# Two-layer model on one core: expert row transfers spread over half steps, routing one batch at a time, and one batch's results fetched at another step

## The chip, the cores and the metric

The kernel runs on one core of one Trainium2 chip. It is written by hand for the core's engines: PE (matrix products into PSUM), VectorE (DVE), ScalarE (ACT), GpSimd (POOL), and SyncE (SP), which here issues most DMA transfers. Each engine works through its own instructions in order; semaphores tie the engines together. The metric is device time in microseconds (us) of one execution.

## The reference

Four batches of 512 tokens with 128 features go through two layers. Each layer normalizes the tokens, computes attention `s` and a feed-forward gate `g` from the same normalized tokens, and adds `s * silu(g)`:

```python
x = L0_attn_x                                  # (4, 512, 128)
xn = _layernorm(x)
s = _L0_attn_ref(xn, ...)   # 16 heads, recurrent over 8 segments of 64 tokens, memory and softmax
g = _silu(_L0_ffn_ref(xn, ...))                # 8 experts, 2 of them per token, and a shared one
x = x + s * g
xn = _layernorm(x)
s = _L1_attn_ref(xn, ...)   # 16 heads of 8, softmax attention summed over 16 channels
g = _silu(_L1_ffn_ref(xn, ...))
x = x + s * g
```

The second layer's experts are what this change is about. Every token takes the two experts with the highest probability, with those two probabilities as weights:

```python
g = gelu(xt @ wg1 + bg1); logits = g @ wg2
probs = softmax(logits); top_vals, top_idx = top_k(probs, 2)
gates = zeros.at[row, top_idx].set(top_vals)
h = gelu(einsum('nd,edh->enh', xt, w_in))      # 8 experts, 128 -> 256
o = einsum('enh,ehd->end', h, w_out)           # 256 -> 128
y = einsum('ne,end->nd', gates, o)
```

## The kernel before

The kernel computes the second layer's experts by rows. It doesn't run all 8 experts over all tokens; it copies each token's row to the two places in DRAM that belong to its two experts, runs each expert over its rows, and fetches each token's two results back. Two halves are treated apart: batches 0 and 1, and batches 2 and 3. An expert has room for 512 rows in each half, so there are 16 pairs of half and expert, called experts 0 to 15 below.

The stages in order of time, by the trace:

- loading, first normalization and the first layer's experts, to about 100 us;
- attention of the first layer (`attn0`), 32 segment steps n, to 422.9 us. The loop runs `attend(n)` and `attended(n - 1)` in each step, and calls what a dictionary `between` holds: an entry n - 0.5 before `attend(n)`, an entry n after `attended(n - 1)`. So work of the second layer's routing is written into steps 18 to 30.5;
- the second layer's experts by rows (`ffn1`), 16 steps i, 422.9 to about 531 us. A second dictionary `between` puts work into the steps: routing of batches 2 and 3, and the preparation (`prepare`) of the second attention's first batch;
- attention of the second layer (`attn1`), 64 steps i = 16 b + t (batch b, t from 0 to 15), 533 to 890 us, and the end.

The order of instructions on every engine is the order in which the program issues them (`pin` and the helpers `mm1`, `act1`, `vec1`, `pool1` and `dma1` record and keep it). So a position in the loop is a position in five queues. Line L322 is the helper of all matrix products, L325 of all ScalarE activations, L334 of transfers issued by SyncE: in the profile one must go by tile names.

The functions of the experts and their names in the profile:

- `sums`, `scale`, `normed`, `turned`: layer normalization of a batch and its transposes (`lnt`);
- `hidden`, `logits`, `chosen`, `placed`: the router of a batch (`pgr`, `lp`, `idx`, `rank`), which ends in `slots` (L1017), the DRAM rows that each token's two copies go to, and `found`, where its results will be;
- `sent(b)` (L1024): eight indirect transfers on GpSimd, four tiles of 128 tokens times two choices. Each scatters 128 rows of 512 bytes from `xn` to the half's DRAM region `in`;
- `fetched(i)`: a 256 KB load of expert i's rows from `in` into `xg` (two buffers), issued by SyncE;
- `faced(i)`: four PE transposes (`xgt`, L1045) and a ScalarE copy (`xt`);
- `up1(i)`: two matrix products (`ph`); `gelu1(i)`: the Gelu into `h` (three buffers in the pool `f1x`);
- `down1(i)`: 16 products (`eo`), a VectorE copy (`y`, L1071), and its 256 KB store to `out`.

The pool `f1x` is opened after `attn0`'s memory is given back, in the same addresses. In step i of `ffn1` before, the order is `up1(i)`, `gelu1(i)`, the entries of `between`, `faced(i + 1)`, `fetched` of a later expert, `down1(i - 1)`.

In `attn1`, at t = 8 of each batch, `back1` issues eight indirect fetches on GpSimd (L1135) from `out`, four for each choice, into `g` and a second tile `bk`. At t = 10 `together` weights and adds them on VectorE (L1145, L1146). At t = 12 `gate1` applies the gate. `zeros1` clears one of two sets of operand strips (L1335) on GpSimd, and `operands1` issues transfers that fill operands.

Of the kernel before, what the change touches and what calls it, by code (L numbers as in the profile page):

```python
# [98 lines left out]
class Kernel:  # L99
# [814 lines left out]
    def begin_ffn1(self, pool, psum, layer):  # L914
# [103 lines left out]
            self.vec1(v.tensor_scalar_min(self.found[:, tiles(b)], row, NE * ROOM - 1.0))  # L1018
            self.vec1(v.tensor_reduce(self.full[:, b : b + 1], rank, AX.XY, ALU.max))

        def sent(b):
            for k in range(4):
                for c in range(2):
                    self.pool1(nc.gpsimd.indirect_dma_start(  # L1024
                        out=self.places[b // 2][b % 2 * 8 + k * 2 + c],
                        out_offset=bass.IndirectOffsetOnAxis(
                            ap=self.slots[:, b * 4 + k, c : c + 1], axis=0
                        ),
                        in_=xn[b][k], in_offset=None,
                    ))  # L1030

        def rows_of(where, i):

# [21 lines left out]
                )  # L1055

        def gelu1(i):
            h = self.f1x.tile([P, 2, 4, P], F32, name=name("h", i), tag="h", bufs=3)
            self.act1(h.rearrange("p c k t -> p c (k t)"), out["h", i], AF.Gelu)
            out["h", i] = h  # L1060

# [46 lines left out]
    def ffn1(self, first, between):  # L1108


        n = 2 * NE
        for i in range(n):
            if i:
                first.up1(i)
            first.gelu1(i)
            for f, *args in between.get(i, []):
                f(*args)
            if i + 1 < n:
                first.faced(i + 1)

            for k in [i + 3] if i + 3 < NE else [NE, NE + 1] if i == NE - 2 else [i + 3] * (
                NE - 2 < i < n - 3
            ):
                first.fetched(k)
            if i:
                first.down1(i - 1)
        first.down1(n - 1)

    def back1(self, b):

        nc, acc = self.nc, self.of_batch("g", 1, b)
        other = self.a1.tile([P, 4, D], F32, name=f"bk{b}", tag="pr1", bufs=2)
        for c, t in enumerate((acc, other)):
            for k in range(4):
                self.pool1(nc.gpsimd.indirect_dma_start(  # L1135
                    out=t[:, k, :], out_offset=None, in_=self.rows_out[b // 2][:],
                    in_offset=bass.IndirectOffsetOnAxis(
                        ap=self.found[:, b * 4 + k, c : c + 1], axis=0
                    ),
                ))  # L1140

        def together():
            for k in range(4):
                w = self.share[:, b * 4 + k]
                self.vec1(nc.vector.tensor_scalar_mul(acc[:, k, :], acc[:, k, :], w[:, 0:1]))  # L1145
                self.vec1(nc.vector.scalar_tensor_tensor(  # L1146
                    acc[:, k, :], other[:, k, :], w[:, 1:2], acc[:, k, :], ALU.mult, ALU.add
                ))
        return acc, together
# [581 lines left out]
    def attn1(self, xnT, g1):  # L1731
# [4 lines left out]
        with tc.tile_pool(name="a1", bufs=2) as self.a1, tc.tile_pool(  # L1736
# [48 lines left out]

            steps = {9: 0, 11: 1, 13: 2, 1: 3}

            def features(b, t):

                out = [(0, t - 1)] if b == 0 and 1 <= t < 5 else []  # L1790
                if t in steps and (b, t) != (0, 1):
                    out.append((b + (t > 1), steps[t]))
                return out
            waiting, late, prep, products = [], [], {}, []
            large = self.large1(flag)
            for i in range(n):
                b, t = i // 16, i % 16
                if i == 0:
                    self.zeros1(1)
                if t == 8:  # L1800
                    g1[b], together = self.back1(b)
                if t == 12:
                    self.gate1(pool, g1[b], b)
                if t % 4 == 2:

                    m = t // 4 + 2
# [27 lines left out]
                    f()  # L1834
                if b == B - 1 and t in (3, 11):
                    large[t // 8]()
                if t == 10:
                    together()
                late = [f for f in [rest(x) for rest, x in ready] if f]
                if nxt:  # L1840
# [301 lines left out]
    def run(self):  # L2142
# [15 lines left out]
        with tc.tile_pool(name="wf1", bufs=1) as wf1, tc.tile_pool(name="f1", bufs=1) as f1:  # L2158
# [11 lines left out]
            with tc.tile_pool(name="ap", bufs=1, space=PSUM) as psum:  # L2170
# [5 lines left out]
                    21: [(first.turned, 0), (first.normed, 1)],  # L2176
                    22: [(first.turned, 1), (first.hidden, 0), (first.hidden, 1)],
                    23: [(first.logits, 0), (first.logits, 1), (first.chosen, 0)],
                    24: [(first.chosen, 1), (first.placed, 0)],
                    25: [(first.placed, 1), (first.sent, 0)], 26: [(first.sent, 1)],  # L2180
                    29: [(first.fetched, 0), (first.fetched, 1)], 30.5: [(first.faced, 0)],
                })
                left[0]()
                first.up1(0)
# [11 lines left out]
                with f1x as self.f1x:  # L2196
# [3 lines left out]
                    def prepare(k):  # L2200
# [2 lines left out]
                        rest(evict[0](ps) if evict else ps)  # L2203

                    self.ffn1(first, {
                        0: [(prepare, 2), (first.sums, 2), (first.sums, 3), (first.scale, 2, 4)],
                        1: [(prepare, 3), (first.normed, 2), (first.turned, 2)],
                        2: [(first.normed, 3), (first.turned, 3), (first.hidden, 2)],
                        3: [(first.hidden, 3), (first.logits, 2), (first.logits, 3),
                            (first.chosen, 2), (first.chosen, 3)],  # L2210
                        4: [(first.placed, 2), (first.sent, 2), (first.placed, 3),
                            (first.sent, 3)],
                        5: [(prepare, 0)], 7: [(prepare, 1), (prepare, 9)],
                        10: [(prepare, 4)], 11: [(prepare, 5)], 12: [(prepare, 6), (prepare, 7)],
                        13: [(prepare, 8)], 14: [(prepare, 10)],
                        15: [(self.opening1, psum, "w", 3)],
# [68 lines left out]
```

## Time and profile before

| what | value |
|---|---|
| median of 3 runs | 915.35 us (912.18 to 916.57) |
| the profiled execution | 915.94 us |
| its span, first to last instruction | 914.1 us |
| mean granted PE clock | 0.959 |
| PE, VectorE, ScalarE, GpSimd busy | 829.5, 594.6, 512.8, 461.6 us |

The profiled execution gives all durations below; it lies 0.6 us above the median. Busy time by stage shows that PE is nearly full everywhere but in the experts by rows:

```profile
core 0: us, PE busy (x) PEld busy (x) DVE busy (x) ACT busy (x) POOL busy (x), PEclk, DMA share, GB/s
0.00:80.00 80.00, 73.42 (x368) 45.97 (x370) 55.43 (x206) 28.42 (x52) 49.66 (x169) 1.00 0.56 155
...
100.00:422.90 322.90, 300.28 (x3595) 257.91 (x3595) 219.56 (x481) 176.34 (x292) 160.46 (x173) 0.96 0.18 52
422.90:533.00 110.10, 90.15 (x545) 63.53 (x545) 30.29 (x119) 37.45 (x47) 40.34 (x43) 0.91 0.32 105
533.00:890.00 357.00, 330.41 (x2612) 114.41 (x2616) 267.08 (x300) 257.31 (x282) 204.47 (x149) 0.97 0.28 87
```

Each row is a stretch of time (its start and end, its length), the busy time of each engine in it with the number of instructions in brackets, the granted PE clock, the mean busy share of the DMA engines and what they moved. The last three rows are the stages that the change touches: the first attention, the experts by rows, and the second attention. A matrix product at half clock takes up to twice its time and counts as busy all of it, so a full PE at a low clock isn't PE at its peak.

### The profile page before, as it was taken

Reading aid. Unit: us, or ns where it says so; the run is one execution under the profiler, and the core shown is the slowest. Engines: PE = TensorE matmul, PEld = TensorE weight load, DVE = VectorE, ACT = ScalarE, POOL = GpSimd, SP = SyncE. Lnnn points to the kernel's source line nnn. Section 1 sums busy time; section 2 is a strip of 40 time slices with the busy share of each in tenths; the row PEclk is TensorE's granted clock in tenths of the full one; section 3 lists DMA queues with packets and bytes.
Section 4 is the critical chain, followed back from the end, with each engine's and each line's share of the span. In section 5 each row is a group of like instructions: output and inputs, shape, how many; then the busy total and the mean of one; then the engine's idle time right before and its main releaser. Section 6 shows DMA issues by size and latency. Waiting matters only on the chain.

```text
span 914.1 us, 18790 instructions
## 1 busy us (share of the span) xinstructions
PE 829.5 (91%) x7428; PEld 505.9 (55%) x7428; DVE 594.6 (65%) x1152; ACT 512.8 (56%) x692; POOL 461.6 (50%) x540
## 2 busy tenths in 40 slices
PE   8998899999999979697968979969999999989896
PEld 4666789888898858585546732322334323422325
DVE  7774776766768785464332236856887887887684
ACT  3434565665656663343512258826776777678670
POOL 7660254454544433755454207973766586551512
PEclk9999999999999998878988999979999999999998
DMA  8822321212212120200523222532251225131000
GB/s 215 260 65 65 88 74 32 82 36 60 82 24 83 25 70 19 61 27 12 189 81 112 82 98 87 196 104 53 70 184 48 81 76 180 54 94 34 24 13 16
DMA packets 85791, 74.42 MB, mean 81 GB/s; under 512 B 41744, under 2 KB 66608, under 8 KB 85696
## 3 DMA queue, kind: packets, MB, share of 16 engines
q1 hardware_dynamic: 81456, 67.52, 24.4%
q0 software_dynamic: 3664, 5.36, 2.2%
q8 instruction: 61, 1.00, 0.4%
q14 instruction: 34, 0.28, 0.1%
q10 hardware_dynamic: 576, 0.26, 0.1%
HBM read 41.66 MB, written 31.46 MB: 80 GB/s over the span
## 4 chain that ended last, share of the span: by engine, by line
PE 64%; DVE 13%; issue 7%; DMA 6%; POOL 4%; ACT 4%; SPq 1%; another core or an unknown queue 1%; DVEq 0%; POOLq 0%; ACTq 0%
PE acc L322 9%; PE pp L322 6%; PE dot L322 6%; PE eo L322 5%; DVE e L1720 5%; PE po L322 5%; PE sc L322 4%; PE mm L322 3%; PE mu L322 3%; PE ph L322 3%; PE pv L322 2%; ACT e L325 2%; DMA other<-qe 2%; PE s L322 2%; PE pk L683 2%
## 5 line engine op out<-in xcount | busy, mean ns | idle before, releaser
L1720 DVE TENSOR_TENSOR e<-e,e 128x1024 f32<-128x1024 f32 x126 | 189.8, 1546 | 68.2 <-ACT e L325 68.1
L322 PE MATMUL acc<-e,strip 128*32 128x512 f32 x1520 | 189.1, 601 | 23.9 <-DVE e L1720 12.2
L325 ACT ACTIVATE e<-s 128x1024 f32<-128x1024 f32 x126 | 122.1, 1022 | 89.7 <-PE s L322 74.9
L325 ACT ACTIVATE e<-e 128x1024 f32<-128x1024 f32 x126 | 126.3, 1060 | 0.0
L322 PEld LDWEIGHTS acc<-e,strip 128*32 128x32 f32 x1520 | 44.6, 110 | 142.0 <-issue 87.2
L325 ACT ACTIVATE pj<-pp 128x512 f32<-128x512 f32 x64 | 38.2, 596 | 65.2 <-PE pp L322 57.5
L776 POOL TENSOR_TENSOR t<-t,gate 128x512 f32<-128x512 f32 x32 | 40.8, 1275 | 54.9 <-DVE t L709 40.2
L322 PE MATMUL dot<-vone,E 128*128 128x65 f32 x512 | 63.2, 277 | 0.6 <-issue 0.5
L322 PEld LDWEIGHTS dot<-vone,E 128*128 128x128 f32 x512 | 61.5, 196 | 1.5 <-issue 1.2
L728 POOL TENSOR_TENSOR t<-t,gate 128x512 f32<-128x512 f32 x32 | 40.9, 1279 | 33.5 <-DVE t L709 33.4
L751 DVE TENSOR_TENSOR mz<-mz,mu 64x512 f32<-64x512 f32 x56 | 38.4, 685 | 22.8 <-PE mu L322 17.4
L647 DVE TENSOR_TENSOR E<-sc,cap 128x1024 f32<-128x1024 f32 x32 | 39.0, 1220 | 16.2 <-PE sc L322 11.6
L325 ACT ACTIVATE attT<-pa 128x512 f32<-128x512 f32 x32 | 19.1, 597 | 54.1 <-PE pa L787 48.9
L671 DVE SCALAR_TENSOR_TENSOR elu<-elu,up 128x512 f32<-128x512 f32 x60 | 42.6, 710 | 7.2 <-ACT up L325 6.4
L1071 DVE COPY y<-eo 128x512 f32<-128x512 f32 x16 | 11.1, 691 | 55.5 <-PE eo L322 41.1
L325 ACT ACTIVATE h<-ph 128x1024 f32<-128x1024 f32 x16 | 16.4, 1024 | 53.5 <-PE ph L322 35.6
L777 POOL TENSOR_TENSOR t<-t,t 128x512 f32<-128x512 f32 x32 | 45.1, 1408 | 2.5
L1024 POOL DMA_INDIRECT in<-xn,slots x32 | 31.8, 995 | 27.0 <-DVE slots L1017 17.9
L744 POOL TENSOR_TENSOR mz<-mz,zs 64x8 f32<-64x8 f32 x56 | 11.7, 208 | 66.4 <-DVE zs L676 57.7
L322 PE MATMUL eo<-w_out,h 128*128 128x128 f32 x256 | 35.1, 295 | 10.1 <-DVE y L1071 8.6
L322 PE MATMUL s<-q,k 32*128 32x512 bf16 x512 | 39.9, 387 | 3.8 <-DMA q<-qd 3.0
L1568 POOL TENSOR_TENSOR pr<-pr,pr 128x512 f32<-128x512 f32 x14 | 21.5, 1552 | 41.7 <-DVE pr L1563 41.7
(303 smaller groups left out, 1771.8 us busy)
## 6 DMA issues: line engine op xcount, KB each, us to landing
vd<-vt SPq DMA_DIRECT2D x32, 256.0 KB
vone<-vd SPq DMA_DIRECT2D x64, 128.0 KB
in<-zero SPq DMA_DIRECT2D x2, 2048.0 KB
xg<-in SPq DMA_DIRECT2D x16, 256.0 KB
out<-y SPq DMA_DIRECT2D x16, 256.0 KB
k<-kd SPq DMA_DIRECT2D x16, 256.0 KB
q<-qd SPq DMA_DIRECT2D x16, 256.0 KB
rows<-qd SPq DMA_DIRECT2D x64, 64.0 KB
```

The lines of the kernel that those rows point to most:

```text
L322: return self.pin(self.nc.tensor.matmul(*args, **kw))
L325: return self.pin(self.nc.scalar.activation(*args, **kw))
L647: self.vec1(nc.vector.tensor_tensor(e.rearrange("p x hp c -> p (x hp) c"), ps.rearrange("p x hp c -> p (x hp) c"), bc(self.cap.rearrange(" ...
L671: self.vec1(nc.vector.scalar_tensor_tensor(t, t, 1.0, up, ALU.min, ALU.add))
L683: self.pin(nc.tensor.transpose(ps[:, hp], src[:, 2 * hp : 2 * hp + 2, :].rearrange("d a j -> d (a j)"), self.ident,))
L728: nc.gpsimd.tensor_mul(t, t, self.gate)
L751: self.vec1(nc.vector.tensor_tensor(new[half, :, :, p, 0:DK], old[half, :, :, p, 0:DK], ps[half, :, :, p * 64 : p * 64 + 64].rearrange("d ...
L776: nc.gpsimd.tensor_mul(t, t, gate2)
L777: nc.gpsimd.tensor_add(t, t, seg[n]["t1"])
L1024: self.pool1(nc.gpsimd.indirect_dma_start(out=self.places[b // 2][b % 2 * 8 + k * 2 + c], out_offset=bass.IndirectOffsetOnAxis(ap=self.slo ...
L1568: self.nc.gpsimd.tensor_add(self.prod1[b, m], self.prod1[b, m], t)
L1720: self.vec1(self.nc.vector.tensor_mul(t, src[0][pair], src[1][pair]))
```

## The change

It has seven parts.

1. In the first attention, the transfers of batches 0 and 1 are no longer issued eight at step 25 and eight at step 26, but two at each half step from 25.5 to 29. The loads of experts 0 and 1 move from step 29 to step 30.
2. The first Gelu's `h` gets memory of its own ("h0") in place of a buffer in `f1x`.
3. In a step of `ffn1`, `faced(i + 1)` comes ahead of the entries of `between`, and the load of a later expert comes after `down1(i - 1)`. Entries of i + 0.5 are called after that. Expert 8 (the first of the second half) is faced at the end of step 7. The loads of experts 8 and 9 move from step 6 to step 7, those of 10 and 11 to step 8.
4. Batches 2 and 3 are routed one after the other, each with its own eight transfers: batch 2's at step 3, batch 3's at step 4.5, where before all 16 were at step 4.
5. `bk` gets one buffer of its own tag; before it shared two buffers with products of the second attention.
6. Batch 0's results are fetched at i = 13, added at 15 and gated at 17, where before this was at 8, 10 and 12. The other batches keep their steps.
7. The clearing of the second operand set moves from the second attention's step 0 to step 9 of `ffn1`.

```diff
--- before.py
+++ after.py
@@ -1018,16 +1018,17 @@
             self.vec1(v.tensor_scalar_min(self.found[:, tiles(b)], row, NE * ROOM - 1.0))
             self.vec1(v.tensor_reduce(self.full[:, b : b + 1], rank, AX.XY, ALU.max))
 
-        def sent(b):
-            for k in range(4):
-                for c in range(2):
-                    self.pool1(nc.gpsimd.indirect_dma_start(
-                        out=self.places[b // 2][b % 2 * 8 + k * 2 + c],
-                        out_offset=bass.IndirectOffsetOnAxis(
-                            ap=self.slots[:, b * 4 + k, c : c + 1], axis=0
-                        ),
-                        in_=xn[b][k], in_offset=None,
-                    ))
+        def sent(b, first=0, end=8):
+
+            for n in range(first, end):
+                k, c = n // 2, n % 2
+                self.pool1(nc.gpsimd.indirect_dma_start(
+                    out=self.places[b // 2][b % 2 * 8 + n],
+                    out_offset=bass.IndirectOffsetOnAxis(
+                        ap=self.slots[:, b * 4 + k, c : c + 1], axis=0
+                    ),
+                    in_=xn[b][k], in_offset=None,
+                ))
 
         def rows_of(where, i):
 
@@ -1055,7 +1056,9 @@
                 )
 
         def gelu1(i):
-            h = self.f1x.tile([P, 2, 4, P], F32, name=name("h", i), tag="h", bufs=3)
+
+            where, tag, bufs = (self.f1x, "h", 3) if i else (pool, "h0", 1)
+            h = where.tile([P, 2, 4, P], F32, name=name("h", i), tag=tag, bufs=bufs)
             self.act1(h.rearrange("p c k t -> p c (k t)"), out["h", i], AF.Gelu)
             out["h", i] = h
 
@@ -1108,28 +1111,34 @@
     def ffn1(self, first, between):
 
 
+
         n = 2 * NE
         for i in range(n):
             if i:
                 first.up1(i)
             first.gelu1(i)
+            if i + 1 < n and i + 1 != NE:
+                first.faced(i + 1)
             for f, *args in between.get(i, []):
                 f(*args)
-            if i + 1 < n:
-                first.faced(i + 1)
-
-            for k in [i + 3] if i + 3 < NE else [NE, NE + 1] if i == NE - 2 else [i + 3] * (
-                NE - 2 < i < n - 3
-            ):
-                first.fetched(k)
             if i:
                 first.down1(i - 1)
+
+            if i + 3 < NE or NE < i < n - 3:
+                first.fetched(i + 3)
+            elif NE - 2 < i <= NE:
+                for k in range(2):
+                    first.fetched(2 * i - NE + 2 + k)
+            for f, *args in between.get(i + 0.5, []):
+                f(*args)
+            if i + 1 == NE:
+                first.faced(NE)
         first.down1(n - 1)
 
     def back1(self, b):
 
         nc, acc = self.nc, self.of_batch("g", 1, b)
-        other = self.a1.tile([P, 4, D], F32, name=f"bk{b}", tag="pr1", bufs=2)
+        other = self.a1.tile([P, 4, D], F32, name=f"bk{b}", tag="bk", bufs=1)
         for c, t in enumerate((acc, other)):
             for k in range(4):
                 self.pool1(nc.gpsimd.indirect_dma_start(
@@ -1785,6 +1794,8 @@
 
             steps = {9: 0, 11: 1, 13: 2, 1: 3}
 
+            back = {16 * b + 8: b for b in range(1, B)} | {13: 0}
+
             def features(b, t):
 
                 out = [(0, t - 1)] if b == 0 and 1 <= t < 5 else []
@@ -1795,12 +1806,12 @@
             large = self.large1(flag)
             for i in range(n):
                 b, t = i // 16, i % 16
-                if i == 0:
-                    self.zeros1(1)
-                if t == 8:
-                    g1[b], together = self.back1(b)
-                if t == 12:
-                    self.gate1(pool, g1[b], b)
+                if i in back:
+                    fb = back[i]
+                    g1[fb], together = self.back1(fb)
+                if i - 4 in back:
+                    fb = back[i - 4]
+                    self.gate1(pool, g1[fb], fb)
                 if t % 4 == 2:
 
                     m = t // 4 + 2
@@ -1834,7 +1845,7 @@
                     f()
                 if b == B - 1 and t in (3, 11):
                     large[t // 8]()
-                if t == 10:
+                if i - 2 in back:
                     together()
                 late = [f for f in [rest(x) for rest, x in ready] if f]
                 if nxt:
@@ -2176,9 +2187,12 @@
                     21: [(first.turned, 0), (first.normed, 1)],
                     22: [(first.turned, 1), (first.hidden, 0), (first.hidden, 1)],
                     23: [(first.logits, 0), (first.logits, 1), (first.chosen, 0)],
-                    24: [(first.chosen, 1), (first.placed, 0)],
-                    25: [(first.placed, 1), (first.sent, 0)], 26: [(first.sent, 1)],
-                    29: [(first.fetched, 0), (first.fetched, 1)], 30.5: [(first.faced, 0)],
+                    24: [(first.chosen, 1), (first.placed, 0)], 25: [(first.placed, 1)],
+                } | {
+                    25.5 + 0.5 * k: [(first.sent, k // 4, k % 4 * 2, k % 4 * 2 + 2)]
+                    for k in range(8)
+                } | {
+                    30: [(first.fetched, 0), (first.fetched, 1)], 30.5: [(first.faced, 0)],
                 })
                 left[0]()
                 first.up1(0)
@@ -2203,14 +2217,16 @@
                         rest(evict[0](ps) if evict else ps)
 
                     self.ffn1(first, {
-                        0: [(prepare, 2), (first.sums, 2), (first.sums, 3), (first.scale, 2, 4)],
-                        1: [(prepare, 3), (first.normed, 2), (first.turned, 2)],
-                        2: [(first.normed, 3), (first.turned, 3), (first.hidden, 2)],
-                        3: [(first.hidden, 3), (first.logits, 2), (first.logits, 3),
-                            (first.chosen, 2), (first.chosen, 3)],
-                        4: [(first.placed, 2), (first.sent, 2), (first.placed, 3),
-                            (first.sent, 3)],
+                        0: [(first.sums, 2), (first.sums, 3), (first.scale, 2, 4)],
+                        0.5: [(prepare, 2), (first.normed, 2), (first.turned, 2)],
+                        1: [(first.hidden, 2), (prepare, 3)],
+                        1.5: [(first.logits, 2), (first.normed, 3)],
+                        2: [(first.chosen, 2), (first.turned, 3)],
+                        2.5: [(first.hidden, 3)],
+                        3: [(first.placed, 2), (first.sent, 2), (first.logits, 3)],
+                        3.5: [(first.chosen, 3)], 4.5: [(first.placed, 3), (first.sent, 3)],
                         5: [(prepare, 0)], 7: [(prepare, 1), (prepare, 9)],
+                        9: [(self.zeros1, 1)],
                         10: [(prepare, 4)], 11: [(prepare, 5)], 12: [(prepare, 6), (prepare, 7)],
                         13: [(prepare, 8)], 14: [(prepare, 10)],
                         15: [(self.opening1, psum, "w", 3)],
```

## The prediction

> **What bounds the kernel now.** I read the page first, then the list of waits, then a table of stretches, then the timeline around two of them, then the chain of waits.
>
> ```profile
> span 914.1 us, 18790 instructions
> ...
> PEclk9999999999999998878988999979999999999998
> ...
> L1024 POOL DMA_INDIRECT in<-xn,slots x32 | 31.8, 995 | 27.0 <-DVE slots L1017 17.9
> ```
>
> PE is busy 91% of the span, so what a row of 40 slices can't show matters: where PE stands, and where its clock is low. The transfers of rows (L1024) are 32 instructions of 0.995 us on POOL. That row's sum, 31.8 us, is small. What happens around them isn't, as the list of waits shows (us in total, times, longest):
>
> ```profile
> POOL in L1024 <- DVE slots L1017: 17.9, 1, 17.9
> ...
> DVE y L1071 <- issue: 14.5, 2, 12.1
> ACT h L325 <- remote: 13.5, 1, 13.5
> ```
>
> POOL waits once 17.9 us for the slots of batch 2 and then issues 16 transfers. VectorE and ScalarE wait 12.1 and 13.5 us at one place for a releaser that the profile can't name ("issue", "remote"). The table of stretches shows where. They are, in order: the transfers of batch 0 and of batch 1 in the first attention, what follows each, the 16 transfers of batches 2 and 3 in the experts, the eight fetches of batch 0's results in the second attention, what follows, and batch 1's fetches for comparison.
>
> ```profile
> core 0: us, PE busy (x) PEld busy (x) DVE busy (x) ACT busy (x) POOL busy (x), PEclk, DMA share, GB/s
> 362.00:374.00 12.00, 6.67 (x80) 5.61 (x76) 5.31 (x9) 3.47 (x6) 9.65 (x11) 0.92 0.11 44
> 378.00:390.00 12.00, 8.60 (x89) 7.20 (x87) 6.23 (x14) 4.33 (x7) 9.67 (x11) 0.93 0.21 66
> 390.00:400.00 10.00, 9.60 (x70) 8.98 (x71) 7.31 (x14) 4.33 (x7) 6.42 (x8) 0.53 0.18 54
> 400.00:415.00 15.00, 14.47 (x196) 13.19 (x192) 11.99 (x25) 5.98 (x9) 7.42 (x8) 1.00 0.00 1
> 472.00:486.00 14.00, 5.42 (x27) 4.18 (x26) 0.69 (x1) 0.45 (x2) 11.46 (x14) 0.71 0.17 66
> 592.00:604.00 12.00, 8.81 (x72) 3.20 (x64) 2.71 (x5) 4.04 (x5) 8.39 (x8) 1.00 0.60 176
> 604.00:622.00 18.00, 12.24 (x48) 4.71 (x52) 14.43 (x24) 8.66 (x10) 10.53 (x6) 0.53 0.13 45
> 682.00:695.00 13.00, 12.60 (x111) 5.94 (x103) 10.26 (x19) 8.15 (x9) 10.14 (x8) 1.00 0.22 66
> ```
>
> In 400–415 PE is full at clock 1.00. In 362–374 and 378–390 it is busy 6.67 and 8.60 of 12 us, in 472–486 5.42 of 14, while POOL is busy with transfers all along, and after them the clock is about half (0.53 in 390–400 and in 604–622). Batch 1's fetches (682–695) leave PE 12.60 of 13 us; batch 0's, with a DMA share of 0.60 against 0.22, don't. The timeline says what ends these stands:
>
> ```profile
> 481.96 0.97 POOL L1024 DMA_INDIRECT in<-xn,slots  x1 [0.30 <-issue]
> 482.81 0.69 DVE L1071 COPY y<-eo 128x512 f32<-128x512 f32 x1 [12.09 <-issue]
> ...
> 485.68 1.02 ACT L325 ACTIVATE h<-ph 128x1024 f32<-128x1024 f32 x1 [13.55 <-remote]
> ...
> 604.53 1.94 ACT L325 ACTIVATE e<-s 128x1024 f32<-128x1024 f32 x2 [8.50 <-remote]
> ...
> 609.37 1.92 PE L322 MATMUL acc<-e,strip 128*32 128x512 f32 x4 [8.56 <-DVE e L1720]
> ```
>
> The copy of y starts as the last transfer of the burst ends (481.96 + 0.97 = 482.93), a Gelu soon after, at 485.68, though what they wait for had been computed some 12 us earlier. After batch 0's fetches ScalarE's exponentials come 8.50 us late and PE's products at 609.37 with them. So from about the fourth to seventh transfer of a burst on, what PE has finished reaches the other engines only when the burst ends. I call this a hold. The chain of waits carries two of them as time with no known releaser:
>
> ```profile
> 367.19 6.40 another core or an unknown queue
> ...
> 471.46 11.36 issue
> ```
>
> **What the Trainium skill says.** "Perfetto Trace Analysis", section "DMA Instruction — SWDGE (GPSIMD)": the profiled window of such a DMA ends when the descriptors are written, not when data moved. The trace agrees: 0.96–1.0 us per transfer, every 1.27 us, and its data landing about 1.1 us later. "SBUF — State Buffer", section "Who interferes with whom", has PE and ACT wait on nobody for memory ports. The trace shows them standing in every long burst, so ports are not the reason, and no page that I read gives one. "TensorE: Matmul & The Clock Gate", section "The HAM clock gate", gives half clock after an idle window of about 3.4 us; the trace has it after each hold, in stretches of 3.4 to 17.1 us, so a hold costs more than its own length.
>
> **The change part by part**, against the profiled execution's 915.94 us (span 914.1), which is 0.6 us above the median of 915.35.
>
> *Transfers of batches 0 and 1, in pairs over eight half steps.* Starts of the value products (dot) of steps 25 to 29: 355.69, 366.70, 380.70, 393.12, 405.61. The four steps 25–28 take 11.0, 14.0, 12.4 and 12.5 us. What PE needs at full clock, from step 29 (5.48) and from a step with output (8.69 in 347.00–355.69), is 8.9, 6.5, 6.0 and 9.5: 30.9 of 49.9 us, so 19 us go to holds and half clock. In the new order POOL has per step L728 1.27 + L744 0.5 + L776 1.27 + L777 1.27 = 4.3 us and two pairs, 4 x 1.27 = 5.1: 9.4 us. Steps 26 and 27 become POOL's: 8.9 + 9.4 + 9.4 + 9.5 = 37.2, so step 29 begins at 392.9, 12.7 us earlier. The last steps then run with POOL behind by some 4 us (the old end, 415.50 to 421.93, is already POOL's t after t): 8.7 left. The fetch of expert 0 moves from step 29 to 30 while its transposes stay at 30.5; a 256 KB load takes 3.1 us to land (the queries' load, 530.54 to 533.65) and half a step is some 2.5, about −1.5 with the issue. Gain about 7 to 8; I take **8**. Bounds: 0 if every pair still holds, 12.7 if the backlog hides. POOL's sums (L776/L777) queue behind each pair, and PE's transposes pa wait for them.
>
> *First Gelu's own memory.* The table load at 430.44 had waited 6.72 us for PE's po and the Gelu ran at 431.74. Both now may go earlier, but the normalization behind it (rstd at 434.65) waits for VectorE's sums until 434.0. Nothing, at most −1.
>
> *Experts: order and routing by batch.* The old stage runs from 422.9 to 531. Steady steps take 3.95 us (transposes 0.44, eo 1.79, ph 1.72). Lost are 11.4 (hold at 471.46), about 2.2 for matmuls at half clock after it, and 3.7 (459.3–463.0, PE waiting for the masks of two batches ranked together): 17 gross. New costs, read from the same rows: two more table loads of 1.28 on ScalarE, which has slack beside matmuls (36 busy of 108 us); and two bubbles at the middle. Expert 8's rows are now fetched behind down1(6), in step 7, and transposed at the end of that same step. SyncE holds the fetch behind y6's store, which waits for the copy: 0.69 + 0.35 issue + 3.1 landing, and PE has nothing else in order: 4 to 4.7 us. Expert 10 is fetched a step later and needs 4.2 us with only up1(9), 1.72, to cover it: 2.3. Together 7. With no holds left the last ph would end near 521.5 instead of 530.66: 17 − 7 − 1 = **−9**. But the transfers still go eight in a row, twice; at 8 the earlier bursts held PE some 4 to 6 us each (6.40 at 367.19), so about +9. Sum **0**, between −9 and +6.
>
> *Batch 0's results at i = 13.* The chain has the eight fetches at 591.90–602.5, 5.32 us for the last to land, then VectorE's e and PE's pl. Step 12 of the attention takes 17.98 us (from its scores at 598.35) and step 13 7.46. The same steps of batch 1 after its fetches take 4.74 and 5.17: 17.98 − 4.74 + 7.46 − 5.17 = 15.5 us. At i = 13 POOL's backlog (its first fetch came 15 us late, behind rows L1495) is gone and stores of y are done, so DMA should be nearer 0.22 than 0.60. Batch 1 still loses about 2.5 near its fetches, which stays: **−13**. Bounds: 0, if the loss moves along with the fetches, to −15.5.
>
> *The rest.* "bk" in its own memory and the zeroing from i = 0 to step 9: it stays behind tsqq in POOL's order, which waits for sizek; 0, ±1.
>
> Sum: −8 + 0 − 13 = −21, so 915.9 − 21 = **895 us**.
>
> **Rivals.**
> *A, no hold in shorter bursts.* Pairs and bursts of eight hold nothing in the new places: the experts give −9 too, and attention 0 may give a few more. 895 − 9 = 886. For it: the first three transfers of a burst never hold. Against: bursts of eight did, 6.4 us.
> *B, only batch 0's results pay.* POOL at 9.4 us per step or a hold at every pair eats the gain in attention 0: 915.9 − 13 = 903. For it: POOL is then full. Against: 9.4 is less than 12 to 14.
> *C, slower.* The hold follows the number of transfers, not their grouping: 32 transfers and 8 fetches cost the same wherever they stand. Then nothing is recovered and the bubbles of experts 8 and 10, 7 us in steps 7 to 9, are left: 923. It decides once less than 7 us of held time come back. For it: every burst had a hold. Against: batch 1's fetches, eight as well, leave PE 12.60 of 13 us.
>
> **How the numbers follow.** Forecast 0.5, A 0.2, B 0.15, C 0.15. A measurement here can tell 0.5%, 4.6 us, from no change. A, B and most of the forecast (it reaches 878 to 908) are faster; its edge and half of C's lower side are within; C is slower at 0.14. So faster 0.78, same 0.08, slower 0.14. The range that leaves out 2 in 10: 878 (A with everything hidden) to 914 (B with the bubbles).
>
> **What would show it.** Right: step 29 of attention 0 begins near 393; no wait above 6 us "remote" in the experts; fetches of batch 0 near 605–615 and no half clock of 17 us after them; a PE gap of 4 to 5 us before expert 8's transposes. Wrong: holds at each pair; attention steps 26–28 still at 12 us; a gap of about 10 us after the fetches at i = 13.

## The result, and the profile after

| | before | changed |
|---|---|---|
| median, 20 runs each | 914.95 us (910.37 to 921.14) | 906.33 us (902.91 to 914.05) |
| ratio | | 0.9924, 95% interval 0.9898 to 0.9949 |
| span of the profiled execution | 914.1 us | 901.3 us |
| mean granted PE clock in it | 0.959 | 0.961 |

By the medians the changed kernel is 8.6 us faster, where some 20 were forecast. The ratio is that of the mean times; by it the gain is 7 us. The profiled executions differ by 12.8 us in span, more than either: the one of the changed kernel is among its fastest (903.04 us), and the one of before has 3 to 4 us in the first attention that other executions don't (see the experiments). The page of the changed kernel has this:

```profile
span 901.3 us, 18771 instructions
...
PEclk9999999999999989985897999999999999999999
...
L1025 POOL DMA_INDIRECT in<-xn,slots x32 | 32.0, 999 | 17.0 <-DVE full L1019 7.9
```

The 32 transfers take what they took, 0.999 us each. The clock is lowest in two slices of 22.5 us: 5 in that of the first attention's end (405.6 to 428.1) and 7 in that of the wait for expert 8 (473.2 to 495.7). The low slices behind the fetches of batch 0's results are gone. In the list of waits (us in total, times, longest) the two of 12.1 and 13.5 us without a known releaser ("issue", "remote") are gone. In their place stand these:

```profile
PE xgt L1046 <- DMA xg<-in: 14.1, 3, 9.7
...
POOL in L1025 <- DVE full L1019: 7.9, 1, 7.9
...
DVE tokq L1377 <- POOL feat L1398: 7.1, 1, 7.1
```

PE waits 9.7 us at one place for the rows of an expert. VectorE waits 7.1 us at one place for GpSimd's products. The table of stretches has, in order: steps 27 and 28 of the first attention, steps 29 and 30 with the last transfers, what follows them, the transfers of batches 2 and 3, the gap before expert 8, and the fetches of batch 0's results at their new place.

```profile
core 0: us, PE busy (x) PEld busy (x) DVE busy (x) ACT busy (x) POOL busy (x), PEclk, DMA share, GB/s
376.00:390.00 14.00, 10.59 (x109) 9.43 (x110) 11.63 (x22) 5.85 (x10) 11.89 (x13) 0.88 0.17 48
390.00:404.00 14.00, 12.38 (x170) 11.34 (x167) 10.82 (x18) 4.51 (x7) 11.80 (x14) 0.99 0.05 20
404.00:416.00 12.00, 9.86 (x54) 8.89 (x53) 6.11 (x14) 2.07 (x4) 7.39 (x7) 0.50 0.24 76
456.00:476.00 20.00, 18.77 (x125) 14.28 (x124) 7.88 (x33) 7.80 (x10) 15.41 (x17) 1.00 0.36 129
478.00:488.00 10.00, 0.39 (x2) 0.42 (x3) 1.29 (x2) 0.00 (x0) 4.80 (x6) 0.71 0.22 79
606.00:620.00 14.00, 14.00 (x122) 4.25 (x124) 10.08 (x14) 11.08 (x13) 10.13 (x9) 1.00 0.31 99
```

In 456–476 all 16 transfers of batches 2 and 3 run back to back, as before, since batch 3's slots are ready at 464.0, before batch 2's eight are out. PE is busy 18.77 of 20 us beside them: no engine is held up. In 606–620 the eight fetches leave PE full. What is new is 478–488, where PE does 0.39 us of work in ten, and 404–416 with a clock of 0.50.

Where the time went, by three marks in the timelines: the dot products of step 25 in the first attention, the product pjk with which the stage of the experts begins, and the first scores of the second attention.

| us | step 25 to the experts | experts | second attention to the end |
|---|---|---|---|
| before | 74.6 | 103.4 | 380.4 |
| changed | 70.8 | 105.0 | 367.9 |

The second attention gives nearly all of it, 12.5 us. A second trace of the changed kernel has 70.9, 105.2 and 371.3 us, so single traces differ by up to 3 us in a stretch.

### The profile page after: what moved, and what is told of

The parts are those of the page before. It is cut to its first block, busy times and chain, and to the rows that moved or that the text cites. A ratio compares the mean times of both kernels' runs of the same rounds, so it can differ in the third digit from the quotient of the medians.

```text
span 901.3 us, 18771 instructions
## 1 busy us (share of the span) xinstructions
PE 824.7 (91%) x7428; PEld 505.1 (56%) x7428; DVE 596.8 (66%) x1152; ACT 515.0 (57%) x694; POOL 462.6 (51%) x540
## 4 chain that ended last, share of the span: by engine, by line
PE 71%; DVE 13%; issue 5%; ACT 4%; POOL 4%; DMA 3%; SPq 0%; DVEq 0%; POOLq 0%; ACTq 0%
PE acc L322 13%; PE pp L322 7%; PE dot L322 6%; PE eo L322 5%; DVE e L1729 5%; PE po L322 5%; PE sc L322 4%; PE ph L322 3%; PE mu L322 3%; PE mm L322 3%; PE s L322 3%; PE pv L322 3%; ACT e L325 3%; PE pl L322 2%; PE pk L683 2%
## 5 line engine op out<-in xcount | busy, mean ns | idle before, releaser
L1729 DVE TENSOR_TENSOR e<-e,e 128x1024 f32<-128x1024 f32 x126 | 183.7, 1498 | 69.8 <-ACT e L325 69.8
L322 PE MATMUL acc<-e,strip 128*32 128x512 f32 x1520 | 186.7, 604 | 13.9 <-DVE bank L1771 10.9
L777 POOL TENSOR_TENSOR t<-t,t 128x512 f32<-128x512 f32 x32 | 45.9, 1435 | 2.5
L325 ACT ACTIVATE E<-E 128x1024 f32<-128x1024 f32 x32 | 33.7, 1052 | 15.1 <-DVE E L647 15.1
```

The source lines that it names most:

```text
L322: return self.pin(self.nc.tensor.matmul(*args, **kw))
L325: return self.pin(self.nc.scalar.activation(*args, **kw))
L777: nc.gpsimd.tensor_add(t, t, seg[n]["t1"])
L1729: self.vec1(self.nc.vector.tensor_mul(t, src[0][pair], src[1][pair]))
```

## Experiments

Sixteen runs in four groups: eleven edits, four of them twice, and the changed kernel once more. Times are medians. The kernels of a group ran on one chip beside the kernel before, whose own median moved from 913.3 to 920.5 us between groups; so the ratio and its interval decide, not the difference of two times. The groups ran on three chips.

### The three parts alone

Results of batch 0 at step 13, on the kernel before:

```diff
-        other = self.a1.tile([P, 4, D], F32, name=f"bk{b}", tag="pr1", bufs=2)
+        other = self.a1.tile([P, 4, D], F32, name=f"bk{b}", tag="bk", bufs=1)
...
+            back = {16 * b + 8: b for b in range(1, B)} | {13: 0}
```

> Only the results of batch 0 are fetched at step 13 (with bk in its own memory); all else as before. Theory 1 (nearly all of the gain is here): 10 us faster than before, about 905, since from the last expert's matmuls to batch 1's fetches the changed kernel's trace is 10 us shorter. Theory 2 (as predicted, three parts share it): 13 us faster. Rival (the loss moves with the fetches and the gain is elsewhere): within 3 us of before.

The spread of batches 0 and 1:

```diff
-                    25: [(first.placed, 1), (first.sent, 0)], 26: [(first.sent, 1)],
-                    29: [(first.fetched, 0), (first.fetched, 1)], 30.5: [(first.faced, 0)],
...
+                    25.5 + 0.5 * k: [(first.sent, k // 4, k % 4 * 2, k % 4 * 2 + 2)]
...
+                    30: [(first.fetched, 0), (first.fetched, 1)], 30.5: [(first.faced, 0)],
```

> Only the row transfers of batches 0 and 1 in pairs over steps 25.5 to 29, and the fetches at 30; all else as before. Theory 1 (GpSimd and the late fetch of expert 0 set the end of the first attention): 2 us faster than before, as the two traces show at the start of the experts. Theory 2 (as predicted): 8 us faster. Rival (the transfers in the steps cost what the bursts cost): no gain, or 2 us slower.

The experts' new order with routing by batch, the first Gelu's memory, and the zeroing at step 9 (parts 2, 3, 4 and 7 of the change, as in its diff):

> Only the new order of the experts, routing by batch and the first Gelu's own memory, with the zeroing at step 9; all else as before. Theory 1 (a gap of 9 to 10 us before expert 8 eats what the missing stand saves): within 2 us of before, 0 to 2 slower by the traces. Theory 2 (as predicted): 0, of a gap of 4 to 5 us and two short holds. Rival (the order saves, and something else in the changed kernel loses): 5 us or more faster.

| part alone | time | ratio, 95% interval | step 25 to experts | experts | second attention |
|---|---|---|---|---|---|
| results at 13 | 905.21 | 0.9904 (0.9878 to 0.9929) | 71.0 | 103.7 | 370.4 |
| spread | 916.27 | 1.0019 (0.9993 to 1.0046) | 70.3 | 103.9 | 383.5 |
| experts | 917.27 | 1.0026 (1.0005 to 1.0048) | 71.3 | 104.6 | 381.5 |

The first alone is the whole gain; the two others give nothing or cost 0.26%. For the spread that is the number of its rival. The last columns add a point. Both kernels with the old bursts take 71.0 and 71.3 us from step 25, not the 74.6 of the trace of before: that trace has 3 to 4 us there that these don't. And their lists of waits show no long wait of VectorE or ScalarE without a releaser. For results at 13, whose experts are unchanged, the list has this instead:

```profile
DVE tokq L1368 <- POOL feat L1389: 11.6, 1, 11.6
PE xgt L1045 <- DMA xg<-in: 8.6, 1, 8.6
```

PE waits 8.6 us for expert 8's rows (476.5 to 485.1 us), in the stretch where before VectorE and ScalarE stood for 12 and 13 us, and the experts take the same 103.7 us. SyncE issues expert 8's load at 482.33, after waiting for the transfers to land (12.0 us between 470 and 490); the last of the 16 was issued at 479.95. So in this order of the experts a stand of the engines during the transfers fills time that would be spent waiting for them.

The first two of these and the changed kernel were repeated together:

> The changed kernel once more, beside the next three. In the traces so far long waits with no named releaser stand in some executions (the kernel before, tokq later with transposes at 31) and in others not (the changed kernel, the three parts alone). Theory 1 (these waits belong to the execution, not to the order of the program): this trace can show some, and the kernel is 8 to 12 us faster than before whether or not. Theory 2 (the changed order takes them away): none here again.

> The spread of batches 0 and 1 alone, once more. Theory 1 (the spread pays only where the waits without a releaser stand at the bursts): where the trace shows such waits, up to 8 us faster than before; where it doesn't, within 3 us of before. Theory 2 (it never pays, since the late load of expert 0 gives it back): within 3 us in either case.

> The results of batch 0 at step 13 alone, once more. Both theories: 9 to 12 us faster than before, and within 3 us of the changed kernel.

Measured: 0.9913 (0.9881 to 0.9945), 1.0001 (0.998 to 1.0022) and 0.9882 (0.9842 to 0.9921). None of the three traces has a long wait of VectorE or ScalarE without a releaser, not even beside the old bursts in results at 13; so theory 1 for the spread, which is about executions with such waits, was not put to the test. They appear in all four traces of one other group (below: no transfers in its first run, additions later, transposes at 31 with tokq later, and loads first in its first run), in both orders of the experts. So they don't come with the order of the program. That group was the only one on its chip, so chip and execution can't be told apart; the chip of the trace of before isn't on record.

### Why the results pay: fetches or additions?

The fetches stay at step 8; only the additions and the gate of batch 0 move, on the kernel before (with bk's own memory):

```diff
-                if t == 12:
-                    self.gate1(pool, g1[b], b)
+                if i in (17, 28, 44, 60):
+                    fb = (i - 12) // 16
+                    self.gate1(pool, g1[fb], fb)
...
-                if t == 10:
+                if i in (15, 26, 42, 58):
                     together()
```

> The kernel before, with bk in its own memory; batch 0's results are fetched at step 8 as before, but added at step 15 and gated at 17. Theory A (VectorE's additions wait for the last fetch and hold up the exponentials' products queued behind them): 8 to 11 us faster than before, as with the fetches moved too. Theory B (the fetches themselves hold up the engines or the memory at step 8): within 3 us of before.

Measured: a ratio of 0.9884 (0.9835 to 0.9934), within its width the same as with the fetches moved too (six executions from 904.33 to 920.98 us, so the median of 913.59 says little). What the additions do at step 10 is seen in the trace of the spread alone, where they stand as before and no long wait of VectorE or ScalarE lacks its releaser. Two lines are of its list of waits, one is of its timeline:

```profile
DVE g L1147 <- DMA bk<-out,found: 7.4, 5, 5.0
...
DVE g L1146 <- DMA g<-out,found: 4.6, 1, 4.6
...
605.60 1.92 PE L322 MATMUL acc<-e,strip 128*32 128x512 f32 x4 [8.61 <-DVE e L1721]
```

VectorE's additions wait 12 us in all for the fetched rows; its products of the exponentials (e, L1721) stand behind them, and PE waits 8.61 us for these. With the additions later the first wait is this:

```profile
DVE g L1146 <- DMA bk<-out,found: 0.9, 2, 0.5
```

Its stretches of the fetches and of what follows:

```profile
core 0: us, PE busy (x) PEld busy (x) DVE busy (x) ACT busy (x) POOL busy (x), PEclk, DMA share, GB/s
592.00:604.00 12.00, 12.00 (x108) 4.01 (x104) 9.77 (x11) 8.18 (x10) 10.47 (x8) 1.00 0.71 209
604.00:622.00 18.00, 17.06 (x112) 5.51 (x104) 10.21 (x14) 11.47 (x13) 8.89 (x7) 0.81 0.25 80
```

The DMA is no less dense than before (share 0.71 against 0.60), yet PE is busy 12.00 of 12 us, and 17.06 of 18 behind them, at clock 0.81 in place of 12.24 at 0.53. So theory A: VectorE's additions at step 10 waited for late fetches, the products of the exponentials queued behind them, and PE ran dry and lost its clock. Nor was it a wait without a releaser: between the copies of the bank ahead of and behind the fetches, the spread alone and the experts alone take 31.9 and 32.2 us, the kernel before 31.9, the results alone 20.3, the additions later 21.3.

Two things are less sure. The stretch after this one takes 29.4 us with the additions later and 24.4 with the results alone, in single traces, so a smaller part of the fetches' own place isn't excluded. And bk's own memory is in all these runs and was not tried alone; no fetch into bk waits longer than 0.3 us, neither where it shares (the spread alone) nor where it doesn't (the results alone).

### What takes the first attention's gain back

The kernel before without the transfers of batches 0 and 1 (the results of these two batches are then not the reference's):

```diff
-                    25: [(first.placed, 1), (first.sent, 0)], 26: [(first.sent, 1)],
+                    25: [(first.placed, 1)],
```

> The kernel before without the 16 row transfers of batches 0 and 1 (the rows of the first half stay zero, so the results of these two batches are not the reference's). Theory 1 (they cost the first attention what the prediction read, 19 us in steps 25 to 28, by standing in GpSimd's queue): step 29 begins near 390 in place of 405.6 and the experts start 12 us or more earlier; 8 to 12 us faster in all, about 905. Theory 2 (the last steps are held by something else): step 29 is early, but the experts start no more than 4 us earlier and the time is within 4 us of before.

> The kernel before without the row transfers of batches 0 and 1, once more (the first half's rows stay zero). Theory 1 (in the attention GpSimd's queue behind the bursts costs nearly the whole of it, with waits without a releaser or without them): the experts start 12 us or more earlier than in any kernel with the bursts, and 8 to 18 us arrive, a ratio of 0.980 to 0.991. Theory 2 (without such waits the bursts cost little): a start less than 5 us earlier, a ratio over 0.995.

Measured: 903.07 us, 0.98 (0.9763 to 0.9837), and in another group 899.0 us, 0.9839 (0.9799 to 0.9879). The chain of the second run:

```profile
388.75 1.74 PE dot L322 x16
...
413.35 1.07 PE pjk L322 x2
```

Step 29's dot products begin at 388.75 and the experts at 413.35; from step 25 it is 57.4 us in both runs. So the transfers cost the first attention 14 us of the 71, and 14 to 18 us arrive at the end. Most of it is PE waiting for GpSimd's sums (t, L777) behind the bursts. Of the two lists of waits, results at 13, with the bursts, is first, and the second run without the transfers is second:

```profile
PE pa L787 <- POOL t L777: 13.9, 4, 6.4
```

```profile
PE pa L787 <- POOL t L777: 3.8, 2, 3.2
```

The prediction's reading that there was much to gain was right. The spread alone keeps step 29 early (38.2 us after step 25, against 46.2 with the results alone) but its chain goes on like this:

```profile
401.70 1.27 POOL t L777
...
403.13 1.00 POOL in L1025
...
404.44 2.26 DMA in<-xn,slots
...
406.76 2.65 DMA xg<-in
...
409.55 1.08 PE xgt L1046 x4
410.63 3.32 PE dot L322 x16
```

The last of GpSimd's sums comes ahead of the last pair of transfers (403.13), these land 2.26 us after their issue, the load of expert 0 waits for them and takes 2.65, and its transposes stand ahead of the last dot products in PE's order. These then run at half clock, 3.32 us in place of 1.74. So the transposes were moved behind them, on the spread alone:

```diff
-                    30: [(first.fetched, 0), (first.fetched, 1)], 30.5: [(first.faced, 0)],
+                    30: [(first.fetched, 0), (first.fetched, 1)], 31: [(first.faced, 0)],
```

> The spread of batches 0 and 1 alone, with expert 0's transposes at step 31 in place of 30.5. Theory 1 (the early steps' gain is lost because PE waits, in front of the last dot, for a load that follows the last transfer): the experts start 4 us earlier than with the spread alone, and 2 to 4 us of it arrive: 912 to 914, a ratio of 0.996 to 0.998. Theory 2 (GpSimd's queue holds the last steps too): no change against the spread alone, a ratio of 1.000.

Measured: 912.35 us, 0.9974 (0.9952 to 0.9996), within theory 1's numbers, though its interval overlaps that of the spread alone. From step 25 it is 64.9 us, 5 less, and the last dot products begin 49.3 us after step 25 in place of 54.3. Some 2 us arrive at the end; where the rest goes isn't shown. What is left in the chain is GpSimd's sums one after another, at the same durations as in the bursts:

```profile
408.41 1.28 POOL t L776
...
409.76 1.05 POOL t L777
...
410.98 1.27 POOL t L728
412.25 1.22 POOL t L776
...
413.56 1.26 POOL t L777
```

### The gap before expert 8

In the changed kernel the timeline before expert 8's transposes is this (the brackets say what ended the idle time before):

```profile
474.85 0.97 POOL L1025 DMA_INDIRECT in<-xn,slots  x1 [0.30 <-issue]
...
478.63 4.24 POOL L1398 TENSOR_TENSOR feat<-tokk 128x512 f32<-128x512 f32 x4
482.91 0.69 DVE L1377 TENSOR_TENSOR tokq<-ptq,l1bqt 128x512 f32<-128x512 f32 x1 [7.08 <-POOL feat L1398]
483.52 0.68 DVE L1074 COPY y<-eo 128x512 f32<-128x512 f32 x1
...
487.61 1.09 PE L1046 MATMUL xgt<-ident,xg 128*128 128x128 f32 x4 [9.67 <-DMA xg<-in]
```

The last transfer ends at 475.82. Behind it in GpSimd's order stand the products of the key tokens (feat), to 482.87; the query tokens (tokq) on VectorE wait for them; the copy of y of expert 6 stands behind tokq; SyncE holds expert 8's load behind the store of that y. So tokq went later, on the changed kernel:

```diff
-                        5: [(prepare, 0)], 7: [(prepare, 1), (prepare, 9)],
+                        5: [(prepare, 0)], 7: [(prepare, 1)], 8.5: [(prepare, 9)],
```

> The changed kernel with the preparation of the query tokens (tokq) moved from step 7 to step 8.5, behind the copy of y of expert 6 and the loads of experts 8 and 9. Theory 1 (the copy of y stands on VectorE behind tokq, tokq behind GpSimd's products, these behind the 16 transfers): the gap before expert 8's transposes falls from 9.7 to about 4 us and the kernel is 5 to 6 us faster than the changed one, about 900. Rival (the load itself is late, or the wait moves to the next step): at most 2 us faster.

Measured: 900.21 us, 0.9847 (0.9808 to 0.9886). The experts take 96.7 us in place of 105.0:

```profile
475.11 0.70 DVE y L1074
...
476.50 2.82 DMA xg<-in
...
479.45 1.10 PE xgt L1046 x4
```

The copy of y is at 475.11, the load leaves at 476.50. Next, the loads ahead of the store, in addition:

```diff
+            if NE - 2 < i <= NE:
+                for k in range(2):
+                    first.fetched(2 * i - NE + 2 + k)
             if i:
                 first.down1(i - 1)
...
-            elif NE - 2 < i <= NE:
-                for k in range(2):
-                    first.fetched(2 * i - NE + 2 + k)
```

> The kernel with tokq later, and the loads of experts 8 and 9 (step 7) and of 10 and 11 (step 8) issued ahead of the store of y rather than behind it. Theory (SyncE holds each load behind a store that waits for VectorE's copy): the gap before expert 8's transposes gets 1 to 2 us shorter, the one before expert 10's 3 us; 3 to 5 us faster than the kernel with tokq later, about 896. Rival (the second half's loads wait for the last transfer anyway): 0 to 1 us.

> Tokq later and the loads first, once more, for comparison on one chip: a ratio of 0.976 as before.

Measured: 899.23 us, 0.9764 (0.974 to 0.9789), and in another group 896.19 us, 0.98 (0.9755 to 0.9845). The experts take 95.5 us in the first, whose trace has waits without a releaser, and 93.7 in the second, 3.0 less than with tokq later alone.

Moving the transposes of expert 0 to step 31 was tried on the kernel with tokq later, and on the one with the loads first:

> The kernel with tokq later, and expert 0's transposes moved from step 30.5 of the first attention to 31, so that they no longer stand ahead of the last dot on PE. Theory (the last pair of transfers, then the load, then these transposes hold up the last two steps, 5 us in the trace): the experts start 3 to 5 us earlier, of which the start of the second attention gives some back; 2 to 4 us faster than the kernel with tokq later, about 897. Rival (the first up product waits for the same rows instead): within 1 us of it, 900.

> The kernel with tokq later and the loads first, and expert 0's transposes at step 31. Theory 1 (the experts start 4 to 5 us earlier and half of it arrives at the end): 2 to 3 us faster than the one with the loads first, some 20 to 22 us faster than before. Rival (the start of the second attention gives all of it back, waiting for GpSimd's rows): the same as the loads first, 0.976 of before.

The first gave 905.65 us, 0.9846 (0.9819 to 0.9873), no better than without. Its trace has the attention shorter, 65.4 us, but two waits without a releaser of 6.1 and 4.6 us in the experts, which take 105.7; so it doesn't decide. The second is the fastest of all, 891.9 us, 0.9743 (0.9705 to 0.978), 67.9 and 93.7 us. Its interval takes in the 0.976 of its rival, so the transposes' own part isn't clear of the noise:

```profile
span 889.7 us, 18771 instructions
...
PE 821.7 (92%) x7428; PEld 503.7 (57%) x7428; DVE 599.9 (67%) x1152; ACT 515.0 (58%) x694; POOL 462.6 (52%) x540
```

Last, this kernel with the transfers of batches 0 and 1 back in two bursts:

```diff
-                    24: [(first.chosen, 1), (first.placed, 0)], 25: [(first.placed, 1)],
+                    24: [(first.chosen, 1), (first.placed, 0)], 25: [(first.placed, 1), (first.sent, 0)],
+                    26: [(first.sent, 1)],
...
-                    25.5 + 0.5 * k: [(first.sent, k // 4, k % 4 * 2, k % 4 * 2 + 2)]
-                    for k in range(8)
```

> The kernel with tokq later, loads first and transposes at 31, but with the transfers of batches 0 and 1 in two bursts at steps 25 and 26 as before. Theory 1 (with the transposes out of the way the spread pays): 3 to 5 us slower than with the spread (0.974), a ratio of 0.978 to 0.980. Theory 2 (the spread pays nothing anywhere): the same, 0.974.

Measured: 897.67 us, 0.9819 (0.9777 to 0.9861), with 71.7 us from step 25. Against 0.9743 in another group that speaks for theory 1, with intervals that just touch. The loads first with the spread measured 0.98 beside it: the spread with early transposes and the bursts with late ones come to the same. That the two have to go together is what this suggests; the bursts with early transposes were not run on this kernel.

## Why the prediction was wrong

**What failed.** Its forecast, 895, was too fast by 11 us. The step that failed is the first term of its sum, "*Transfers of batches 0 and 1, in pairs over eight half steps*", taken at 8 us and measured at nothing (1.0019 and 1.0001). Its sum for the spread's own steps was near: 37.2 us from step 25 to step 29, measured 38.2. That is 8.0 us earlier than with the results alone (46.2), where the prediction had 12.7, since the 49.9 us of the trace of before stand only in traces with waits without a releaser (50.2 with the additions later; 46.0 to 46.3 in the four traces with the same bursts and no such wait). And of these 8.0 the last steps took back 7.3, where it priced some 4 for GpSimd's backlog and 1.5 for the load. It let the load of expert 0 wait only for its own position, and not for the last transfer, which that same spread had moved from step 26 to step 29; and it left out that the transposes, which wait for this load, stand ahead of the last dot products in PE's order.

**The hold.** The prediction rested on a mechanism read from one trace, that from the fourth to seventh transfer on PE's results reach nobody until the burst ends. The changed kernel's 16 transfers of batches 2 and 3 stand in one stretch without any such thing, and so do the old bursts in the runs of single parts. What the bursts cost in the traces without such waits is plainer: GpSimd's own sums, which stand behind them in its queue, and the loads that wait for the last one. The first is shown by PE's wait of 13.9 us for these sums, which falls to 3.8 without the transfers, the second by PE's wait of 8.6 us for expert 8 where no engine was held. In the trace of before the wait for these sums is 3.8 us too, since PE stands at other places there. The prediction named the sums in GpSimd's queue, but only behind the new pairs.

**The experts.** The sum was 0 and the part alone is 0.26% slower, about 2 us: near, for the wrong reasons. The hold of 9 us didn't come. The bubble of 4 to 4.7 us before expert 8 was 9.7: the working counted the copy of y as 0.69 us and overlooked that tokq stands ahead of it on VectorE, and GpSimd's products and 16 transfers ahead of tokq. It also assumed two bursts of eight; they are one of sixteen, since batch 3's slots are ready 8.3 us after the first transfer, before the eight are out. Expert 10's wait, priced at 2.3 (its own figures, 4.2 less 1.72, give 2.5), is 2.30.

**Batch 0's results.** Forecast −13, measured 0.9904 and 0.9882, some 9 to 11 us; the right part and direction, a size off by a quarter. The cause that it named, POOL's backlog and a dense DMA, made the fetches late, but only the additions that wait for them on VectorE turned this into a loss: their place alone gives the same within the width of the runs.

**The rivals.** Rival B, that only batch 0's results pay, at 903, is what happened; it was given 0.15. Its reason, that GpSimd becomes the bound of the attention at 9.4 us per step, holds for its end, where GpSimd's sums follow one another in the chain; the spread's own steps did get shorter. C's bubble was real, but too small against the results. The range, 878 to 914, held the time.

**What stays open.** Where the waits without a releaser come from. In the trace of before and in the four that show them, three to four tenths of the landing records of GpSimd's transfers are missing (1141 to 1308 of some 1800, and 1102 of 1545 without the transfers); the other traces have nearly all, and none of these waits. Where they appear the traces are longer: with the old bursts by some 4 us from step 25 to step 29, and the experts with tokq later took 105.7 us with them against 96.7 without. Whether they belong to the chip, to single executions or to the recording, no run here tells.

## What to carry to other kernels

When a transfer that many things wait for is spread out to relieve its queue, its last piece moves later: find the first reader of the whole, and everything that stands behind that reader on each in-order engine. Before pricing a wait as a copy plus a load, walk back the queue of the engine that makes the copy; here four queues in a row (GpSimd, VectorE, SyncE, PE) turned 4 us into 10. And a stand that appears in one execution is worth a second trace of the same code before a sum is built on it: here some 4 us of the first term were such.

## What the runs showed of the hardware that was not expected

With the transfers between GpSimd's sums, a pair of small operations on VectorE (sums, L771, 128x8) takes 1.44 and 2.03 us in steps of the spread in place of 0.24 (with the old bursts, in results at 13, at most 0.96); in the changed kernel one ends as GpSimd's work does (398.71 to 400.65, beside GpSimd from 398.67 to 400.62). "SBUF — State Buffer", section "Who interferes with whom", in the Trainium skill gives a reason: VectorE's second port pair is GpSimd's, under an exclusive lock. That this is the reason here was not tried.

Sixteen indirect transfers back to back, one every 1.27 us, left PE 18.77 of 20 us busy at full clock; in the trace of before sixteen of them stood beside a standstill of VectorE of 12.09 us. The order of instructions did not tell which.
